# Gated MLP on transposed data: inverse roots broadcast through DRAM, the mean taken out of the first weights, and a reordered beginning

## The chip, the cores and the metric

The kernel runs on one core of a Trainium2 chip. The metric is the device time of one execution in microseconds (us), the median of three runs. The core has five engines with an instruction queue each: PE (TensorE, matmuls and transposes), DVE (VectorE), ACT (ScalarE), POOL (GpSimd) and SP (SyncE, which here only issues DMAs). Each engine works through its own queue in order, so an instruction that waits holds up everything queued behind it on that engine.

## The reference

The input x has 16 batches of 512 tokens with 128 features. A vector of modulations (scales, shifts, gates) is made from `c`. Cut to what matters:

```python
h = _layernorm(x) * (1 + ca) + sa
x = x + ga * _L0_attn_ref(h, ...)        # causal attention, 16 heads of 8
h = _layernorm(x) * (1 + cb) + sb
x = x + gb * _L0_ffn_ref(h, ...)         # the block below
# _L0_ffn_ref: two layers, each
x = x + local_attention(shift(x)) @ wo   # 8 heads of 64, window 64
h = shift_token(x)
mu, var = h.mean(-1), h.var(-1)
h = (h - mu) / sqrt(var + 1e-05) * lg + lb
a, g = split(h @ w1 + b1)                # 341 columns each
x = x + (a * gelu(g)) @ w2 + b2
```

The second half of each layer, from `mu, var` on, is called the MLP here. The first part of the change concerns it.

## The kernel before, in words

**Stage 1** (0 to about 640 us) is the causal attention, in units of a batch's heads, four units for each of the 16 batches. `stage_a` normalises a batch, transposes it, projects it to q and k, splits them into bf16 parts and writes these to DRAM (`qd`, `kd`; L269 is the line of all loads and stores that go through `load`). `load_stack` reads them back as the stacks `qst` and `kst`; rows 48 and 49 of each half of `kst` hold the constant −1, which `new_stack` sets with a memset of 32 rows (L486). `prep_mod`, `prep_gates` and the rest of `prep_...` make the modulations and the folded weights, in the order written out by hand ahead of the planner: batch 0's `stage_a` steps (`head[...]`) stand among them.

**Then two layers** (640 to 2008 us), each a local attention over the 16 batches (`proj_steps`, `chunk_steps`, `out_steps`) followed by the MLP over the 16 batches (`mlp_steps`). In layer 0 the attention takes about 640 to 1185 us and the MLP 1185 to 1305 us; in layer 1 the attention takes 1290 to 1865 us, and the MLP goes to the end.

**The residual stream** lies transposed in `ys`, 128 features on the partitions and 16 × 512 tokens along the free axis. The MLP's matmuls want their input this way, but mean and variance of a token are a reduction over partitions, so the kernel transposes:

- `stat_steps` (batches 0 to 13, beside the attention): four PE transposes, `bn_stats`/`bn_aggr` on DVE, and for every second batch an inverse root on ACT and POOL. It leaves mean and inverse root of each token as columns in SBUF.
- `mlp_steps`, step f1: four PE transposes of `ys` to tokens-on-partitions (L1197) and four DVE `tensor_scalar` of 128×128 that subtract the mean and multiply by the inverse root (L1188). For the last two batches (14 and 15, one pair) f1 makes the statistics too: transposes (L1209), `bn_aggr` (L1215), a bit trick for the inverse root on DVE (L1219 to L1221), three Newton rounds on POOL (12 small operations, L1225 to L1228), then the eight L1188 of both batches.
- f2: four PE transposes back (L1236), an ACT cast to the high part (L156), a DVE subtract for the low part (L1240).
- Three `gate` and three `up` steps (gelu on ACT; L1260 on DVE, a cast on ACT, L1265 on POOL), three `down` steps, then two DVE additions into `ys` (L1286). The last layer adds f5: scaling on ACT, four transposes (L1303), an addition of `x1` (L1305), the store of the output.

A product of full precision (`mm3`) is three fp32r matmuls of 128×512 (L867 to L869): high·high, high·low, low·high. A batch of the MLP has nine `mm3`, 27 matmuls.

**What sets the order.** `Plan.due(t, steps)` gives each step a due time, and the steps are emitted in order of these; the framework's scheduler then places the instructions on each engine. `MT` holds the due times of the MLP's steps in units of `UM` us from a batch's own start, `MTL` that of f1 of the late pair, `t1` the start of the MLP. Tiles from `flat("r")` and the like rotate through a fixed number of buffers (`FB`), `third(tag)` through three banks of PSUM, `ps_s()` through three others.

`weights_mlp` loads the MLP's weights, folds `ln_g` and `ln_b` into the first and splits them into high and low parts.

Of the kernel before, what the change touches and what calls it, by code (L numbers as in the profile page):

```python
# [35 lines left out]
LW, LWD = (2.8, 0.169)  # L36
LP0, LP1 = (-3.063, 0.706)

MT = (-2.0, -1.044, -0.081, 0.079, 0.264, 0.82, 0.69, 1.583, 0.71, 0.968, 1.97, 2.863)

EARLY, LS = 14, (0.3, 0.9)

MTL = -4.8

UA, UC, UM = (8.3, 8.033, 7.042)
GA, GM, GL = (0.037, 2.139, 0.75)

FB = (2, 2, 2, 2, 3, 6, 5, 4)
# [37 lines left out]
def kernel(  # L86
# [155 lines left out]
    for first in (False, True):  # L242
# [11 lines left out]
            nc.gpsimd.memset(m[0:64, 0:64], -NEG)  # L254
        masks.append(m)


    ys = const.tile([128, B, T + 1], F32, name="ys")
    nc.vector.memset(ys[64:128, :, 0:1], 0.0)
# [5 lines left out]
    wts = ctx.enter_context(tc.tile_pool(name="wts", bufs=1))  # L265
    weights = [{} for _ in range(DEPTH)]

    def load(**k):
        return tc.keep_in_program_order(nc.sync.dma_start(**k))  # L269

    def split(src, shape, name):
# [59 lines left out]
    def weights_mlp(l):  # L331
        W = weights[l]
        st_ = {}

        def f1():
            lg = wts.tile([128, 2], F32, tag="lg", name="lg")
            load(out=lg[:, 0:1], in_=ln_g[l].unsqueeze(1))
            load(out=lg[:, 1:2], in_=ln_b[l].unsqueeze(1))
            bb = W["b"] = wts.tile([128, 7], F32, tag="bb", name="bb")
            nc.gpsimd.memset(bb, 0.0)  # L340
            load(out=bb[:, 6:7], in_=b2[l].unsqueeze(1))
            for j in range(2):
# [12 lines left out]
        def g1():  # L355
            t, lg, bb = st_["1"], st_["lg"], W["b"]
            p = bank("m", BK[2])
            for i in range(6):
                nc.tensor.matmul(p[:, i : i + 1], lhsT=t[:, i, :], rhs=lg[:, 1:2], start=True, stop=True)
            nc.vector.tensor_tensor(bb[:, 0:6], bb[:, 0:6], p[:, 0:6], ALU.add)  # L360
            nc.vector.tensor_scalar(t, t, lg[:, 0:1], None, ALU.mult)
            W["1"] = split(t, [128, 6, 128], "w1")

        def f2():
            t = stage([128, 3, D])
            nc.gpsimd.memset(t, 0.0)
# [115 lines left out]
    def new_stack(i):  # L482
        q_ = at.tile([128, NH // 4, T], BF, name=f"qst{i}")
        k_ = at.tile([128, NH // 4, T], BF, name=f"kst{i}")
        for par in range(2):
            nc.gpsimd.memset(k_[64 * par + 32 : 64 * par + 64], -1.0)  # L486
        qst.append(q_)
        kst.append(k_)

# [36 lines left out]
    def stage_a(b):  # L526
# [29 lines left out]
        def put(key):  # L556
            def f():

                sp = s[key]
                d = dram.tile([6, HD, NH, T], BF, tag=key + "d", bufs=3, name=key + "d")  # L560
                for o, n, part in ((0, 3, 0), (3, 2, 1), (5, 1, 2)):
                    src = sp[:, 0:n] if key == "kd" else sp[:, part : part + 1].to_broadcast([128, n, T])
                    load(out=d[o : o + n].rearrange("s d h t -> (d h) s t"), in_=src)
                s[key] = d

            return f
# [19 lines left out]
    def load_stack(i):  # L586
        b, half = divmod(i, 2)
        for par in range(2):
            rows = slice(64 * par, 64 * par + R0)
            hs = slice(8 * par + 4 * half, 8 * par + 4 * half + 4)  # L590
            for st_, key in ((qst, "qd"), (kst, "kd")):
                load(out=st_[i % NS][rows], in_=st[b][key][:, :, hs, :].rearrange("s d h t -> (s d) h t"))

    def stacks(u):
        j = 2 * (u % 2)
# [553 lines left out]

    z_ = {}  # L1150

    mvs, rss = {}, {}

    def stat_steps(l, b):
        def f1():
            if b == 0:
                mvs[l] = small("lmv", [128, EARLY, NB, 2], 1)
            p = third("m")
            for n in range(NB):
                nc.tensor.transpose(p[:, n * 128 : (n + 1) * 128], ys[:, b, n * 128 : (n + 1) * 128], ident)  # L1160
            s6 = small("ms6", [128, NB, 6], 1)
            for n in range(NB):
                nc.vector.bn_stats(s6[:, n, :], p[:, n * 128 : (n + 1) * 128])
            for n in range(NB):
                nc.vector.bn_aggr(mvs[l][:, b, n, :], s6[:, n, :])

        def f2():
            if b % 2 == 0:
                return
            ve = small("lve", [128, 2, NB], 2)  # L1170
            nc.gpsimd.tensor_scalar(ve, mvs[l][:, b - 1 : b + 1, :, 1], EPS, None, ALU.add)
            rs, nwt = rsqrt_steps(pool["wk"], ve, [128, 2, NB], "ls", nc.gpsimd, EARLY // 2)
            for f in nwt:
                f()
            for i in range(2):
                rss[l, b - 1 + i] = rs[:, i, :]

        return [f1, f2]

    def mlp_steps(l, b):  # L1180
# [1 line left out]
        W = weights[l]  # L1182
        s = {}

        def normalised(p, b, mv, rs):
            z = z_[l, b] = flat("r").rearrange("p (n d) -> p n d", n=NB)
            for n in range(NB):
                nc.vector.tensor_scalar(  # L1188
                    z[:, n, :], p[:, n * 128 : (n + 1) * 128], mv[:, n, 0:1], rs[:, n : n + 1], ALU.subtract, ALU.mult
                )  # L1190

        def f1():
            if b < EARLY:

                p = ps_s() if b < 2 else third("e")
                for n in range(NB):
                    nc.tensor.transpose(p[:, n * 128 : (n + 1) * 128], ys[:, b, n * 128 : (n + 1) * 128], ident)  # L1197
                normalised(p, b, mvs[l][:, b], rss[l, b])
                return

            if b % 2 == 1:
                return
            s6 = small("mt6", [128, 2, NB, 6], 1)
            mv = small("mmv", [128, 2, NB, 2], 1)
            rs = small("mrs", [128, 2, NB], 1)
            ps = [third("e") for _ in range(2)]
            for i, p in enumerate(ps):
                for n in range(NB):
                    nc.tensor.transpose(  # L1209
                        p[:, n * 128 : (n + 1) * 128], ys[:, b + i, n * 128 : (n + 1) * 128], ident  # L1210
                    )
                for n in range(NB):
                    nc.vector.bn_stats(s6[:, i, n, :], p[:, n * 128 : (n + 1) * 128])
                for n in range(NB):
                    nc.vector.bn_aggr(mv[:, i, n, :], s6[:, i, n, :])  # L1215

            ve = small("mve", [128, 2, NB], 1)
            nt = small("mnt", [128, 2, NB], 1)
            nc.vector.tensor_scalar(ve, mv[:, :, :, 1], EPS, None, ALU.add)  # L1219
# [4 lines left out]
            for _ in range(3):  # L1224
# [1 line left out]
                nc.gpsimd.tensor_tensor(nt, nt, ve, ALU.mult)  # L1226
                nc.gpsimd.tensor_scalar(nt, nt, -0.5, 1.5, ALU.mult, ALU.add)
                nc.gpsimd.tensor_tensor(rs, rs, nt, ALU.mult)  # L1228
            for i, p in enumerate(ps):
                normalised(p, b + i, mv[:, i], rs[:, i])  # L1230

        def f2():
            p = ps_s() if b < 1 else third("e")
            z = z_.pop((l, b))
            for n in range(NB):
                nc.tensor.transpose(p[:, n * 128 : (n + 1) * 128], z[:, n, :], ident)  # L1236
            zh = flat("t1").bitcast(F32R)
            zl = flat("t2").bitcast(F32R)
            copy(11, zh, p)
            nc.vector.tensor_tensor(zl, p, zh.bitcast(F32), ALU.subtract)  # L1240
            s["zT"] = zh, zl

        def gate(i):
# [66 lines left out]
        steps = [f1, f2]  # L1310
        for i in range(3):
            steps += [gate(i), up(i)]
        steps += [down(i) for i in range(3)]
# [59 lines left out]
    for l in range(DEPTH):  # L1373
# [84 lines left out]
```

## Time and profile before

| what | value |
|---|---|
| median of 3 runs | 2010.7 us (2007.6 to 2011.55) |
| the profiled execution: its own time | 2010.06 us |
| its span, first to last instruction | 2008.3 us |
| mean granted PE clock over the span | 0.979 |
| stretch 640 to 1150 us (layer 0 attention) | PE 472.45, DVE 447.62, ACT 449.67 of 510.00 us |
| stretch 1185 to 1264 us (layer 0 MLP) | PE 78.34, DVE 58.42, ACT 48.61, POOL 49.54 of 79.00 us |
| stretch 1264 to 1277 us | PE 7.09 of 13.00 us, clock 0.75 |
| stretch 1885 to 1949 us (layer 1 MLP) | PE 64.00, DVE 51.52, ACT 44.72, POOL 30.03 of 64.00 us |
| stretch 1949 to 1964 us | PE 9.60 of 15.00 us, clock 0.77 |

The profiled execution has 1.76 us outside its span. A busy time is the time in which an engine was working, without the issuing of DMAs. Matmul durations overlap each other (one of 0.39 us is followed by the next after 0.23 us), so the cost of a matmul is read from the starts. In the rows of a timeline the columns are start, duration, engine, line, operation, output and inputs, shape and number merged into the row; in brackets stands how long the engine was idle before it and what ended that. SPq, DVEq and the like are the engines' queues: DMA issues and waits.

### The profile page before, as it was taken

How to read it: one execution, taken by the hardware profiler on the slowest of the kernel's cores; microseconds unless marked ns; L12 is line 12 of the kernel's file. 1: busy time of each engine (PE TensorE's matmuls, PEld its weight loads, DVE VectorE, ACT ScalarE, POOL GpSimd, SP SyncE). 2: the span in 40 equal slices, each digit the busy share in tenths (PEclk: the TensorE clock that was granted, in tenths of full speed). 3: DMA queues.
4: the chain of work that ended last, by engine and by line, in shares of the span. 5: the costliest groups of instructions: out<-in, count | busy, mean ns of one | idle time of the engine just before them, and what ended most of it. 6: DMA issues, size and time to landing. Idle time of an engine off the chain costs nothing. (4 is left out here: it accounts for less than half of the span.)

```text
span 2008.3 us, 55061 instructions
## 1 busy us (share of the span) xinstructions
PE 1810.0 (90%) x20474; PEld 1238.3 (62%) x20474; DVE 1631.2 (81%) x4851; ACT 1588.6 (79%) x4218; POOL 1319.2 (66%) x1916
## 2 busy tenths in 40 slices
PE   5899899898898799999999989889999899989998
PEld 3444444444444577777677768666767676767776
DVE  5788888888885888888888967698888888887686
ACT  2587777777787889999899875578889888888766
POOL 5345555555456878887878746587887777775444
PEclk8799999999999999999999999999999999999999
DMA  4445545545541211101010200020101010101022
GB/s 122 101 105 155 149 109 151 130 118 133 120 103 50 51 38 24 39 20 38 21 39 20 54 2 18 1 45 20 42 21 39 20 38 20 39 20 26 27 73 64
DMA packets 96904, 120.68 MB, mean 60 GB/s; under 512 B 16626, under 2 KB 79612, under 8 KB 94588
## 3 DMA queue, kind: packets, MB, share of 16 engines
q1 hardware_dynamic: 96156, 116.62, 24.1%
q8 instruction: 162, 2.65, 0.6%
q14 instruction: 106, 0.87, 0.1%
q10 hardware_dynamic: 480, 0.54, 0.1%
HBM read 48.43 MB, written 38.81 MB: 43 GB/s over the span
## 5 line engine op out<-in xcount | busy, mean ns | idle before, releaser
L174 ACT ACTIVATE pr<-pr,m 128x128 f32<-128x128 f32 x1024 | 408.9, 406 | 44.3 <-DVE m L1054 41.9
L627 DVE TENSOR_REDUCE mx<-ps_w 128x2 f32<-128x1024 f32 (+3 forms) x448 | 389.8, 911 | 62.2 <-PE ps_w L617 61.9
L953 POOL TENSOR_TENSOR r<-t,t 128x512 f32<-128x512 f32 x256 | 327.6, 1283 | 98.0 <-DVE t L944 65.2
L944 DVE TENSOR_TENSOR t<-ps_s,tab 128x512 f32<-128x512 f32 x512 | 327.8, 681 | 59.7 <-ACT sq L940 37.0
L174 ACT ACTIVATE pt<-ps_w 128x1024 f32<-128x1024 f32 x320 | 323.9, 1025 | 59.8 <-PE ps_w L706 55.4
L717 POOL TENSOR_SCALAR_AFFINE_SELECT pt<-pt 128x256 f32<-128x256 f32 (+1 forms) x448 | 190.7, 440 | 219.5 <-ACT pt L174 216.7
L1054 DVE CUSTOM_DVE_ANT_0 pr<-ps_e,maskl,rky 128x128 f32<-128x128 f32 x1024 | 295.5, 344 | 29.6 <-PE ps_e L1033 26.2
L1082 POOL TENSOR_TENSOR pr<-pr,den 128x512 f32<-128x512 f32 x256 | 265.6, 1041 | 76.7 <-DVE den L1081 70.3
L930 PE MATMUL ps_s<-wqh,hh 128*128 128x512 f32 x384 | 177.7, 463 | 36.2 <-DVE t L944 24.1
L174 ACT ACTIVATION_READ_ACCUMULATOR pr<-pr,m 128x1 f32 x1024 | 205.9, 201 | 0.0
L1265 POOL TENSOR_TENSOR kT<-pr,qT 128x512 fp32r<-128x512 f32 x96 | 123.0, 1292 | 121.5 <-ACT qT L156 121.2
L766 PE MATMUL ps_m<-pt,vau 128*32 128x512 f32 (+3 forms) x2048 | 197.4, 451 | 0.4 <-POOL pt L717 0.4
L1033 PE MATMUL ps_e<-kT,qT 64*64 64x128 f32 (+1 forms) x4608 | 180.1, 272 | 12.7 <-DVE m L1054 7.2
L950 DVE TENSOR_REDUCE ss<-sq 128x8 f32<-128x512 f32 x256 | 171.5, 675 | 2.1 <-ACT sq L940 2.1
L607 PE MATMUL ps_w<-kst,qst 48*128 48x512 bf16 (+3 forms) x1024 | 150.4, 310 | 21.3 <-ACT pt L174 11.3
L940 ACT ACTIVATE sq<-ps_s 128x512 f32<-128x512 f32 x256 | 150.1, 596 | 21.3 <-PE ps_s L932 17.1
L1033 PEld LDWEIGHTS ps_e<-kT,qT 64*64 64x64 f32 x4608 | 122.1, 133 | 68.1 <-issue 24.2
L706 PE MATMUL ps_w<-qst,kst 50*128 50x512 bf16 (+3 forms) x1024 | 126.4, 304 | 39.8 <-DVE mx L627 38.0
L931 PE MATMUL ps_s<-wql,hh 128*128 128x512 f32 x384 | 153.6, 400 | 0.0
L932 PE MATMUL ps_s<-wqh,hl 128*128 128x512 f32 x384 | 153.0, 399 | 0.0
L617 PEld LDWEIGHTS <-idm 64*128 64x128 bf16 x2048 | 103.8, 98 | 56.6 <-issue 26.7
L977 POOL TENSOR_TENSOR r<-r,rky 128x512 f32<-128x512 f32 x128 | 131.7, 1044 | 3.7
(244 smaller groups left out, 4244.9 us busy)
## 6 DMA issues: line engine op xcount, KB each, us to landing
v<-v SPq DMA_DIRECT2D x32, 512.0 KB
qst<-qdd SPq DMA_DIRECT2D x64, 192.0 KB
kst<-kdd SPq DMA_DIRECT2D x64, 192.0 KB
v<-v SPq DMA_DIRECT2D x32, 384.0 KB
qdd<-qd SPq DMA_DIRECT2D x16, 384.0 KB
kdd<-kd SPq DMA_DIRECT2D x16, 384.0 KB
od<-o SPq DMA_DIRECT2D x128, 36.0 KB
xt<-in_L_attn_x_dram SPq DMA_DIRECT2D x16, 256.0 KB
```

The costliest lines, as they stand in the source:

```text
L174: ins = nc.scalar.activation(*a, **k)
L627: nc.vector.tensor_reduce(dst, src, AX.X, ALU.max)
L717: nc.gpsimd.affine_select(v, v, pattern=[[0, n], [1, 128]], compare_op=ALU.is_ge, fill=0.0, base=0, channel_multiplier=-1)
L766: mm_ = nc.tensor.matmul(p[32 * hl : 32 * hl + 32, kb * 128 : T], lhsT=va[:, kb, h * 9 : h * 9 + 32], rhs=pts[hl, seg][:, off : off + n], ...
L930: nc.tensor.matmul(p, lhsT=hh[:, cols], rhs=wqh[:, wc], start=True, stop=False)
L931: nc.tensor.matmul(p, lhsT=hh[:, cols], rhs=wql[:, wc], start=False, stop=False)
L944: nc.vector.tensor_tensor(t, pv, W["tab"][:, n, 2 * j + k, :].unsqueeze(1).to_broadcast([128, LH, LD]), ALU.mult,)
L950: nc.vector.tensor_reduce(loc["ss"][:, n - n0, j, :], sq, AX.X, ALU.add)
L953: nc.gpsimd.tensor_tensor(r.rearrange("p h (x d) -> p h x d", x=2), t1.rearrange("p h (x d) -> p h x d", x=2), t2.rearrange("p h (x d) -> ...
L1033: nc.tensor.matmul(later["e"][64 * w : 64 * w + 64, par, hp * 128 + o : hp * 128 + o + n], lhsT=s["q"][r0 : r0 + 64, hp, q0 + 64 * w : q0 ...
L1054: nc.vector.tensor_tensor_reduce(pr[:, i, :], later["e"][:, par, hp * 128 : (hp + 1) * 128], mk, s["rq", cc][:, 2 * hp + par : 2 * hp + pa ...
L1082: nc.gpsimd.tensor_tensor(pr, pr, den.unsqueeze(2).to_broadcast([128, 4, 128]), ALU.mult)
```

## The change

1. **The MLP no longer transposes its input.** The mean of the tokens is removed by the weights: `weights_mlp` subtracts from each column of the folded first weights its mean over the 128 features (a matmul with a matrix of 1/128, two times 384 columns, and a DVE subtraction each). What remains per token is a factor, the inverse root. `put_roots` writes it to DRAM (`rsd`, one row of 512 per batch) with one DMA per batch from SP, in single elements of 4 bytes. f1 is now a DMA that reads the row back, broadcast to 128 partitions (256 KB, into `flat("sq")`, which has two buffers); f2 is one DVE product of 128×512 of `ys` and this tile, then the cast and the subtraction as before, now from SBUF.
2. **The statistics of the late pair** move into a new step f0 with the due time `MTL`; its inverse roots go through DRAM like the others. Its `z` is made in f2, no longer with the statistics.
3. **Due times and buffers:** the first entry of `MT` goes from −2.0 to −3.0, `UM` from 7.042 to 6.0, `t1` is bounded by f0 of the late pair; `up` takes its bank from `third("e")` from batch 2 on.
4. **The beginning:** the eight memsets of `kst` on POOL become eight small DMAs from SP of two rows each; `new_stack` and `head[0]` (normalisation of batch 0) go ahead of `prep_silu` and `prep_mod`, `head[5]` and `head[6]` (projections, `qd`/`kd`) ahead of `prep_mod(2, 5)` and `prep_gates`; for batch 0 the writes of `kd` and the loads of `kst` are issued by ACT.

```diff
-MT = (-2.0, -1.044, -0.081, 0.079, 0.264, 0.82, 0.69, 1.583, 0.71, 0.968, 1.97, 2.863)
+MT = (-3.0, -1.044, -0.081, 0.079, 0.264, 0.82, 0.69, 1.583, 0.71, 0.968, 1.97, 2.863)
-UA, UC, UM = (8.3, 8.033, 7.042)
+UA, UC, UM = (8.3, 8.033, 6.0)
...
+    ones = const.tile([128, 128], F32, name="ones")
+    nc.gpsimd.memset(ones, 1.0 / D)
...
             nc.vector.tensor_scalar(t, t, lg[:, 0:1], None, ALU.mult)
+            for j in range(2):
+                p = bank("m", BK[2])
+                tj = t[:, 3 * j : 3 * j + 3, :].rearrange("p i n -> p (i n)")
+                nc.tensor.matmul(p[:, 0:384], lhsT=ones, rhs=tj, start=True, stop=True)
+                nc.vector.tensor_tensor(tj, tj, p[:, 0:384], ALU.subtract)
             W["1"] = split(t, [128, 6, 128], "w1")
...
         for par in range(2):
-            nc.gpsimd.memset(k_[64 * par + 32 : 64 * par + 64], -1.0)
+            nc.sync.dma_start(
+                out=k_[64 * par + R0 : 64 * par + R1], in_=minus.unsqueeze(1).to_broadcast([2, NH // 4, T])
+            )
...
-                    load(out=d[o : o + n].rearrange("s d h t -> (d h) s t"), in_=src)
+                    load(b == 0 and key == "kd", out=d[o : o + n].rearrange("s d h t -> (d h) s t"), in_=src)
...
+    def put_roots(l, b, rs):
+        for i in range(2):
+            nc.sync.dma_start(out=rsd[l][b + i].rearrange("(n p) -> p n", p=128), in_=rs[:, i, :])
...
-        def normalised(p, b, mv, rs):
-            z = z_[l, b] = flat("r").rearrange("p (n d) -> p n d", n=NB)
-            for n in range(NB):
-                nc.vector.tensor_scalar(
-                    z[:, n, :], p[:, n * 128 : (n + 1) * 128], mv[:, n, 0:1], rs[:, n : n + 1], ALU.subtract, ALU.mult
-                )
-        def f1():
-            if b < EARLY:
-                p = ps_s() if b < 2 else third("e")
-                for n in range(NB):
-                    nc.tensor.transpose(p[:, n * 128 : (n + 1) * 128], ys[:, b, n * 128 : (n + 1) * 128], ident)
-                normalised(p, b, mvs[l][:, b], rss[l, b])
+        def f0():
+            if b < EARLY or b % 2 == 1:
                 return
+            for i in range(2):
+                variance(l, b + i, third("e"))
...
-            for i, p in enumerate(ps):
-                normalised(p, b + i, mv[:, i], rs[:, i])
+            put_roots(l, b, rs)
+
+        def f1():
+            s["rs"] = flat("sq")
+            nc.sync.dma_start(out=s["rs"], in_=rsd[l][b].unsqueeze(0).to_broadcast([128, T]))
         def f2():
-            p = ps_s() if b < 1 else third("e")
-            z = z_.pop((l, b))
-            for n in range(NB):
-                nc.tensor.transpose(p[:, n * 128 : (n + 1) * 128], z[:, n, :], ident)
+            z = flat("r")
+            nc.vector.tensor_tensor(z, ys[:, b, 0:T], s["rs"], ALU.mult)
             zh = flat("t1").bitcast(F32R)
             zl = flat("t2").bitcast(F32R)
-            copy(11, zh, p)
-            nc.vector.tensor_tensor(zl, p, zh.bitcast(F32), ALU.subtract)
+            copy(11, zh, z)
+            nc.vector.tensor_tensor(zl, z, zh.bitcast(F32), ALU.subtract)
...
-                p = ps_s()
+                p = ps_s() if b < 2 else third("e")
...
+    minus = pp.tile([2, T], BF, name="minus")
+    nc.gpsimd.memset(minus, -1.0)
     if B > 1:
         load_x(1)
+    for i in range(NS):
+        new_stack(i)
     head = stage_a(0)
+    head[0]()
     prep_silu()
     prep_mod(0, 2)
-    head[0]()
     prep_q()
     prep_k()
     for f in head[1:4]:
         f()
+    head[5]()
+    head[6]()
     prep_mod(2, 5)
     prep_gates()
-    head[5]()
-    head[6]()
-    for i in range(NS):
-        new_stack(i)
...
-        t1 = max(t0 + 4 * B * UC + GM, freed - UM * (B - 1 + MT[0]) + 0.1)
+        t1 = max(t0 + 4 * B * UC + GM, freed - UM * (B - 2 + MTL) + 0.1)
-            for t, f in zip(MT, lazy(lambda l=l, b=b: mlp_steps(l, b), 11 + int(last))):
-                due(t1 + UM * (b + (t if b < EARLY or t != MT[0] else MTL)), [f])
+            for t, f in zip((MTL,) + MT, lazy(lambda l=l, b=b: mlp_steps(l, b), 12 + int(last))):
+                due(t1 + UM * (b + t), [f])
```

`variance(l, b, p)` holds the four transposes, `bn_stats` and `bn_aggr` that `stat_steps` and the late pair had written out. In the loads of `load_stack`, `b == 0 and key == "kd"` is passed in the same way, and `load(True, ...)` issues from ACT.

More of the change, by code (lines that the diff above doesn't have):

```diff
@@ L266, with load @@
     weights = [{} for _ in range(DEPTH)]
-    def load(**k):
+    def load(other=False, **k):
+        if other:
+            return nc.scalar.dma_start(**k)
         return tc.keep_in_program_order(nc.sync.dma_start(**k))
@@ L591, in load_stack @@
             for st_, key in ((qst, "qd"), (kst, "kd")):
-                load(out=st_[i % NS][rows], in_=st[b][key][:, :, hs, :].rearrange("s d h t -> (s d) h t"))
+                load(b == 0 and key == "kd", out=st_[i % NS][rows], in_=st[b][key][:, :, hs, :].rearrange("s d h t -> (s d) h t"))
     def stacks(u):
@@ L1150, with variance @@
     z_ = {}
-    mvs, rss = {}, {}
+    rsd = [dram.tile([B, T], F32, name=f"rsd{l}") for l in range(DEPTH)]
+    mvs = {}
+    def put_roots(l, b, rs):
+        for i in range(2):
+            nc.sync.dma_start(out=rsd[l][b + i].rearrange("(n p) -> p n", p=128), in_=rs[:, i, :])
+    def variance(l, b, p):
+        if b % 2 == 0:
+            mvs[l, b] = small("lmv", [128, 2, NB, 2], 2)
+        mv = mvs[l, b - b % 2][:, b % 2]
+        for n in range(NB):
+            nc.tensor.transpose(p[:, n * 128 : (n + 1) * 128], ys[:, b, n * 128 : (n + 1) * 128], ident)
+        s6 = small("ms6", [128, NB, 6], 2)
+        for n in range(NB):
+            nc.vector.bn_stats(s6[:, n, :], p[:, n * 128 : (n + 1) * 128])
+        for n in range(NB):
+            nc.vector.bn_aggr(mv[:, n, :], s6[:, n, :])
     def stat_steps(l, b):
         def f1():
-            if b == 0:
-                mvs[l] = small("lmv", [128, EARLY, NB, 2], 1)
-            p = third("m")
-            for n in range(NB):
-                nc.tensor.transpose(p[:, n * 128 : (n + 1) * 128], ys[:, b, n * 128 : (n + 1) * 128], ident)
-            s6 = small("ms6", [128, NB, 6], 1)
-            for n in range(NB):
-                nc.vector.bn_stats(s6[:, n, :], p[:, n * 128 : (n + 1) * 128])
-            for n in range(NB):
-                nc.vector.bn_aggr(mvs[l][:, b, n, :], s6[:, n, :])
+            variance(l, b, third("m"))
         def f2():
@@ L1170, in f2 @@
             ve = small("lve", [128, 2, NB], 2)
-            nc.gpsimd.tensor_scalar(ve, mvs[l][:, b - 1 : b + 1, :, 1], EPS, None, ALU.add)
-            rs, nwt = rsqrt_steps(pool["wk"], ve, [128, 2, NB], "ls", nc.gpsimd, EARLY // 2)
+            nc.gpsimd.tensor_scalar(ve, mvs.pop((l, b - 1))[:, :, :, 1], EPS, None, ALU.add)
+            rs, nwt = rsqrt_steps(pool["wk"], ve, [128, 2, NB], "ls", nc.gpsimd, 2)
             for f in nwt:
                 f()
-            for i in range(2):
-                rss[l, b - 1 + i] = rs[:, i, :]
+            put_roots(l, b - 1, rs)
         return [f1, f2]
@@ L1183, in mlp_steps @@
         s = {}
-        def normalised(p, b, mv, rs):
-            z = z_[l, b] = flat("r").rearrange("p (n d) -> p n d", n=NB)
-            for n in range(NB):
-                nc.vector.tensor_scalar(
-                    z[:, n, :], p[:, n * 128 : (n + 1) * 128], mv[:, n, 0:1], rs[:, n : n + 1], ALU.subtract, ALU.mult
-                )
-        def f1():
-            if b < EARLY:
-                p = ps_s() if b < 2 else third("e")
-                for n in range(NB):
-                    nc.tensor.transpose(p[:, n * 128 : (n + 1) * 128], ys[:, b, n * 128 : (n + 1) * 128], ident)
-                normalised(p, b, mvs[l][:, b], rss[l, b])
+        def f0():
+            if b < EARLY or b % 2 == 1:
                 return
[L1201 to L1204, printed above, removed]
+            for i in range(2):
+                variance(l, b + i, third("e"))
+            ve = small("lve", [128, 2, NB], 2)
+            nt = small("mnt", [128, 2, NB], 1)
             rs = small("mrs", [128, 2, NB], 1)
-            ps = [third("e") for _ in range(2)]
-            for i, p in enumerate(ps):
[L1208 to L1219, printed above, removed]
+            nc.vector.tensor_scalar(ve, mvs.pop((l, b))[:, :, :, 1], EPS, None, ALU.add)
             nc.vector.tensor_scalar(nt.bitcast(I32), ve.bitcast(I32), 1, None, ALU.logical_shift_right)
@@ L1228, in f1 @@
                 nc.gpsimd.tensor_tensor(rs, rs, nt, ALU.mult)
-            for i, p in enumerate(ps):
-                normalised(p, b + i, mv[:, i], rs[:, i])
+            put_roots(l, b, rs)
+        def f1():
+            s["rs"] = flat("sq")
+            nc.sync.dma_start(out=s["rs"], in_=rsd[l][b].unsqueeze(0).to_broadcast([128, T]))
         def f2():
-            p = ps_s() if b < 1 else third("e")
-            z = z_.pop((l, b))
-            for n in range(NB):
-                nc.tensor.transpose(p[:, n * 128 : (n + 1) * 128], z[:, n, :], ident)
+            z = flat("r")
+            nc.vector.tensor_tensor(z, ys[:, b, 0:T], s["rs"], ALU.mult)
             zh = flat("t1").bitcast(F32R)
             zl = flat("t2").bitcast(F32R)
-            copy(11, zh, p)
-            nc.vector.tensor_tensor(zl, p, zh.bitcast(F32), ALU.subtract)
+            copy(11, zh, z)
+            nc.vector.tensor_tensor(zl, z, zh.bitcast(F32), ALU.subtract)
             s["zT"] = zh, zl
@@ L1308, in f5 @@
             )
-        steps = [f1, f2]
+        steps = [f0, f1, f2]
         for i in range(3):
```

## The prediction

> **What bounds the kernel now.** I read the page's busy shares first, then a table by stage, because the shares are a mean over stages with different limits.
>
> ```profile
> PE 1810.0 (90%) x20474; PEld 1238.3 (62%) x20474; DVE 1631.2 (81%) x4851; ACT 1588.6 (79%) x4218; POOL 1319.2 (66%) x1916
> ```
>
> PE leads, but only by 9 points. Four slices of 7 us, as columns length, PE, PEld, DVE, ACT, POOL, granted clock, DMA share and GB/s, say more:
>
> ```profile
> 1178.00:1185.00 7.00, 4.12 (x65) 3.34 (x66) 4.04 (x21) 6.14 (x22) 2.41 (x3) 1.00 0.01 2
> 1206.00:1213.00 7.00, 7.00 (x34) 5.70 (x33) 4.69 (x7) 4.60 (x7) 2.27 (x3) 1.00 0.00 0
> 1220.00:1227.00 7.00, 7.00 (x36) 5.73 (x35) 6.89 (x14) 4.54 (x8) 4.83 (x5) 1.00 0.03 7
> 1269.00:1276.00 7.00, 3.79 (x12) 2.71 (x13) 4.63 (x13) 0.58 (x1) 0.67 (x4) 0.61 0.00 0
> ```
>
> In the MLP (rows 2 and 3) PE is full, so removed PE work is removed time. In the passage from attention to MLP (row 1) nothing is full: a chain of DVE, ACT, POOL and PE. At the late pair (row 4) PE stands and its clock falls. These three places, and the first 40 us, are what the change touches.
>
> **1. Transposes out of a full PE.** The timeline of PE in layer 0:
>
> ```profile
> 1246.84 0.39 PE L868 MATMUL ps_m<-kT,w2h 128*128 128x512 f32 x1
> 1247.07 0.39 PE L869 MATMUL ps_m<-qT,w2l 128*128 128x512 f32 x1
> 1247.30 0.60 PE L1209 MATMUL ps_x<-ident,ys 128*128 128x128 f32 x4
> 1247.65 0.48 PE L867 MATMUL ps_s<-t,w1h 128*128 128x512 f32 x1
> 1247.97 0.39 PE L868 MATMUL ps_s<-t,w1h 128*128 128x512 f32 x1
> ```
>
> A matmul costs 0.23 us from start to start. Four transposes and the matmul after them take 1247.30 to 1247.97, 0.67, so four transposes cost 0.44 and one 0.11. A batch of layer 0 is now 27 × 0.233 + 8 × 0.11 = 7.18 us, and 6.30 after; layer 1 (four more transposes in f5) goes from 7.62 to 6.74. Removed per layer are 14 × 8 + 2 × 4 = 120 transposes; I leave out the 16 of batches 0 and 1, which fall in the unfilled passage. So 2 × 104 × 0.11 = **−23 us**, −26 if all count.
>
> It holds only if no other engine is near 6.3. DVE per batch loses four L1188 of 0.40 (1.6 in sum, 1.37 pipelined) and gains one product of 128×512 in f32, which is nearest to L1240 (0.69): 0.69 + 0.69 + 3 × 0.75 (L1260) + 2 × 0.75 (L1286) = 5.1, and 5.8 with L1305 in layer 1. ACT: 3 × 0.68 (gelu) + 3 × 0.62 + 0.58 = 4.5, about 6.0 with f5. POOL 3 × 1.29 = 3.9. All are below 6.30 and 6.74, but DVE and ACT in layer 1 by little; were they the bound by queueing, half of the gain would go (−11).
>
> **2. The late pair.** Its L1188 wait for POOL's Newton rounds:
>
> ```profile
> 1269.95 1.37 DVE L1188 TENSOR_SCALAR r<-ps_x,mmv,mrs 128x128 f32<-128x128 f32 x4 [2.59 <-POOL mrs L1228]
> ...
> 1271.38 1.12 PE L1197 MATMUL ps_x<-ident,ys 128*128 128x128 f32 x4 [3.94 <-DVE r L1188]
> ...
> 1273.80 0.58 ACT L156 CAST t<-ps_e 128x512 fp32r<-128x512 f32 x1 [8.50 <-PE ps_e L1236]
> ```
>
> The bracket of row 1 names POOL, of row 2 the DVE queue behind it: an earlier batch's L1188 stands behind the late pair's eight, so PE starves and restarts slow. In 1264 to 1277 PE issues 23 instructions: 10 transposes and 13 matmuls, worth 1.1 + 3.0 = 4.1 us at full clock, so 8.9 of 13 us are lost. In 1949 to 1964 (layer 1) 34 instructions, 16 and 18, are worth 6.0: 9.0 of 15 lost. Together 17.9.
>
> After the change the DVE instruction that waits is the pair's product `z`, and between inverse root and `z` there are more links. In the order of the new kernel's DVE seven operations (about 5.1 us) stand between the bit trick (`nt`, `rs` in f0) and `z` of batch 14 in layer 0, ten (7.4 us) in layer 1. The chain: 1.3 until POOL starts (1265.3 to 1266.6) + 3.3 Newton + two put issues 0.7 + landing 1.5 + a load 2.9 + its issue 0.4, about 10 us. The bounds of the unknown links are these rows, two of stage 1's DRAM trip and one of the last chain:
>
> ```profile
> 318.40 0.34 SPq L269 DMA_DIRECT2D rdd<-rd  x1
> ...
> 319.87 0.59 SPq L269 DMA_DIRECT2D rb<-rdd  x1
> ```
>
> ```profile
> 2001.47 2.87 DMA v<-x1d
> ```
>
> A write to DRAM had landed by 1.5 us after its issue, and a load of the same 256 KB took 2.87. So DVE stalls 5 us in layer 0 and 3 in layer 1; PE has 2 to 4 us of matmuls queued, and loses about 3 and 1: 17.9 − 4 = **−14 us** (−17 if covered, −5 if both stalls reach PE in full and the clock falls).
>
> The clock: PE idle 3.94 us here, granted 0.61 in the slice, matmuls 0.43 apart. The Trainium skill (TensorE: Matmul & The Clock Gate, Part 1) puts the fall to half clock after an idle window of about 3.4 us. By it my 3 us in layer 0 keep the clock with little room; past it a dozen matmuls 0.43 apart in place of 0.23 would add 2.4.
>
> **3. The beginning.** The timeline, first POOL and DVE, then SP's queue, then the first use of scores:
>
> ```profile
> 4.33 14.85 POOL L486 MEMSET kst<- 32x2048 bf16 x8
> 14.70 2.74 DVE L522 TENSOR_SCALAR xn<-xt,mv,rsy 128x128 f32<-128x128 f32 x4
> ```
>
> ```profile
> 26.80 0.32 SPq L473 DMA_DIRECT2D gad<-ga  x1
> 27.22 1.57 SPq L269 DMA_DIRECT2D qdd<-qd  x3
> ```
>
> ```profile
> 39.68 3.55 DVE L627 TENSOR_REDUCE mx<-ps_w 128x2 f32<-128x1024 f32 x4 [3.16 <-PE ps_w L617]
> ```
>
> The x of batch 0 has its first `bn_stats` at 5.21, its last at 11.6, behind the modulations' chain; then L522 takes 2.74 beside POOL's memsets (1.11 for batch 1 without them). `qd` is ready at 23.8 but its write waits behind `gad` until 27.2, and the first `kst` load goes at 33.4. With `head[0]` first, no memsets and no `gad` ahead, I put `hT` at 12 (18.2 now), the writes at 20 to 21, the loads' end at 26, first maximum at 27 to 30. That is −10 to −12; but batch 1's projections, which now come behind the first scores on PE, and ACT, which now issues seven DMAs (0.3 to 0.6 each by SP's rows), may give some back, and so may PE's clock, granted 0.50 from 40 to 70. I take **−9 us** (−12 to −4). Everything in stage 1 then moves by that.
>
> The Trainium skill speaks against part of it: DMA: Bandwidth & Descriptors (Issuing engines are not separate DMA queues) says that a second issuing engine saves only the issue time. No run here shows two at once on this path; by it ACT's seven issues are worth no more than the 3 us or so that they took on SP.
>
> **4. What the DRAM trip costs in the passage.** `z` of batches 0 to 7 stands on DVE between the last attention chunks, in order. A load into `sq` can be issued only when the `z` two batches before is done, and lands 3.3 us later (0.4 + 2.9); on SP it also stands behind the next layer's 768 KB of weights (layer 0) and the puts of pair 12/13. Where `z` waits, the chunk's L1054 behind it waits, then ACT's exp, then the gelu, which cannot start until the last exp. Below: nothing, or a gain of 2.7 (batches 0 and 1 lose their L1188, 1.37 each). Above: two waits of 3.3 a layer and a slow put, 7 a layer. I take **+8 us** for both layers, nearer the upper end, since row 1 of the slices shows no engine with work to spare there (bounds −3 to +14).
>
> **5. Additions.** Two products with `ones` per layer, f32, 384 columns: a pair of f32 products of 512 columns took 2.07 in the beginning (at low clock), so at most 0.8 each, and two subtractions of about 0.55 on DVE, which delay the weights' split; +0 to +3, I take **+2**. Sixteen loads and puts per layer run where the DMA share is 0.0 to 0.25. SP holds nothing else that is urgent there but the output stores of layer 1. A put is 512 runs of 4 bytes per batch, where stage 1's was of 256 bytes; no row of before has that at size, so its landing may be twice the 1.5 us, which is in the bounds of steps 2 and 4.
>
> **Sum.** −23 − 14 − 9 + 8 + 2 = −36. From the profiled execution's own 2010.06 that is 1974; the median of the runs is 0.6 above, hence **1975 us**. All bounds at their good end give −26 − 17 − 12 − 3 = −58 (1953); all at their bad end −11 − 5 − 4 + 14 + 3 = −3 (2007).
>
> **Rivals.**
>
> *The trip through DRAM gives half of it back (1992).* For it: DVE works in order, two buffers, SP's queue, the short passage. Then the passage costs +14 and the late pair saves only 5 with the head at −8: −23 − 5 − 8 + 14 + 3 = −19, from 2010.06 to 1991, by the median 1992, some 1985 to 2000. Against: in steady state a load has two periods, 12.6 us, for 3.3.
>
> *Slower.* One mechanism: the loads through two `sq` buffers become a chain that paces the MLP. `z` of a batch waits for a load that is issued after the `z` two before, so the period cannot be less than half of issue-to-use. It decides from 12.6 us per trip; at 2 × 7.8 = 15.6 the batches take 1.5 us more than my 6.30, 32 × 1.5 = 48 against the 36 saved: 2022. A trip of 3.3 by the rows above would have to be almost five times as long, by small puts or SP's queue. Unlikely.
>
> *Another engine takes over (1986).* DVE or ACT in layer 1 by queueing, or the banks that `up` now shares with the statistics: −11 in place of −23 gives 1986.
>
> *The MLP doesn't gain at the end* since its last batches wait for attention's last: excluded, the last attention output is long done when PE is full at 1206.
>
> **Chances.** Forecast (1962 to 1984) 0.62; half given back 0.16; another engine 0.12; slower 0.07; the rest, within 0.2% (4 us, about what a measurement of this kernel can tell from no change), 0.03. The 8-in-10 range leaves out the slower case and the tails: 1957 to 1999. Faster by over 0.2%: 0.90; within: 0.03; slower: 0.07.
>
> **What would show it.** Right: first L627 before 31; a table by stage with PE full in both MLPs and 6.3 and 6.7 us between the additions into `ys`; at the late pair a gap of PE under the 3.94 us of now and the clock near 1.00; in the passage waits of DVE for the DMA of `sq`, 3 us at most. Wrong: periods over 7 with DVE waiting on `sq`; a PE gap at the late pair as long as before; L627 early but the second batch's scores late.

## The result, and the profile after

The changed kernel takes 2039.4 us (median of 4 runs, 2038.1 to 2042.2) against 2009.5 of the kernel before (4 runs, 2007.6 to 2011.55): a ratio of 1.015, 95% interval 1.0133 to 1.0168. It is slower by 30 us where 36 us less were forecast. The profiled execution has a span of 2037.9 us.

Where the time went is read first from milestones in the traces (us from the span's start; `den` is the reciprocal that each half of a local attention chunk takes on DVE, `ys` the first of the two additions of the MLP's last batch into the residual stream). The last two columns are experiments told of below. Stage 1 alone, of the same instructions, ends up to 9.2 us apart between traces, and a later stage varies by some 3 us, so differences of that size say little.

| milestone | before | changed | `after_put32` | `rows` |
|---|---|---|---|---|
| first maximum of the scores | 39.7 | 32.9 | 33.2 | 32.5 |
| last maximum of stage 1 (its start) | 612.8 | 605.4 | 606.6 | 604.2 |
| last `den`, layer 0 | 1183.2 | 1216.0 | 1193.2 | 1180.4 |
| last batch's `ys`, layer 0 | 1320.4 | 1354.4 | 1321.6 | 1306.0 |
| last `den`, layer 1 | 1864.0 | 1894.2 | 1845.6 | 1839.4 |
| end | 2008.3 | 2037.9 | 1981.6 | 1970.7 |

The changed kernel is 7.4 us ahead when stage 1 ends, and 32.8 behind when the attention of layer 0 ends. Its two MLPs, from the last `den` on, take 138.4 and 143.7 us against 137.2 and 144.3: no gain is seen there, though the transposes are gone.

The page of the changed kernel, busy times of the engines, then a table by stage (columns as in the prediction):

```profile
PE 1802.6 (88%) x20242; PEld 1222.6 (60%) x20242; DVE 1623.6 (80%) x4759; ACT 1587.1 (78%) x4218; POOL 1320.1 (65%) x1910
```

```profile
640.00:1150.00 510.00, 457.89 (x5507) 348.39 (x5507) 426.82 (x1589) 431.32 (x1459) 391.54 (x498) 0.97 0.15 31
1185.00:1220.00 35.00, 22.97 (x285) 17.52 (x284) 15.88 (x75) 21.64 (x75) 8.90 (x11) 0.80 0.27 62
1293.00:1312.00 19.00, 10.79 (x44) 7.75 (x43) 6.41 (x12) 6.97 (x12) 7.85 (x16) 0.90 0.11 29
1972.00:1992.00 20.00, 10.05 (x40) 6.71 (x37) 8.28 (x12) 7.59 (x12) 7.13 (x10) 0.80 0.55 53
```

In 640 to 1150, where only attention runs, every engine is less busy than before (PE 457.89 against 472.45, DVE 426.82 against 447.62) although its instructions there are nearly the same: they wait more. The other rows are the passage of layer 0 and the two late pairs, with PE idle for 8 to 12 us in each.

What they wait for at a late pair is told by the chain of waits in layer 1 (start, duration, what):

```profile
1973.63 0.21 POOL mrs L1226
...
1973.86 10.68 DMA rsd<-mrs
...
1984.56 3.45 DMA sq<-rsd
```

The load (3.45) is near the 2.87 that the prediction took; the write of 2 × 512 roots takes 10.68 us, where the prediction took 1.5. At the late pair of layer 0 the issues of the write and of the next load stand at 1297.19 and 1307.72, 10.53 apart. The waits that follow, first DVE's, then PE's:

```profile
1195.48 0.69 DVE L1235 TENSOR_TENSOR r<-ys,sq 128x512 f32<-128x512 f32 x1 [6.62 <-DMA sq<-rsd]
...
1310.97 1.29 DVE L1235 TENSOR_TENSOR r<-ys,sq 128x512 f32<-128x512 f32 x2 [10.02 <-DMA sq<-rsd]
...
1875.64 0.69 DVE L1235 TENSOR_TENSOR r<-ys,sq 128x512 f32<-128x512 f32 x1 [7.17 <-DMA sq<-rsd]
```

```profile
1989.56 0.79 PE L881 MATMUL ps_e<-t,w1h 128*128 128x512 f32 x1 [9.14 <-DVE pr L1259]
```

Rows 1 and 3 are the passages, behind the write of pair 12/13; row 2 is the late pair.

In the attention nothing waits for a root, and yet time goes. The place of one of the seven writes in layer 0, on SP, PE and DVE:

```profile
961.18 0.92 SPq L1171 DMA_DIRECT2D rsd<-lsy  x2
975.88 0.47 SPq L1020 DMA_DIRECT2D v<-v  x1
```

```profile
967.64 0.56 PE L1125 MATMUL ps_m<-pT,v 128*64 128x64 f32 x10
969.33 0.22 PE L1125 MATMUL ps_m<-pT,v 128*64 128x64 f32 x1 [1.13 <-issue]
972.45 0.27 PE L1125 MATMUL ps_m<-pT,v 128*64 128x64 f32 x1 [2.90 <-issue]
```

```profile
972.66 0.35 DVE L1068 CUSTOM_DVE_ANT_0 pr<-ps_e,maskl,rky 128x128 f32<-128x128 f32 x1 [4.20 <-remote]
```

PE stops in the middle of a group of matmuls, with no releaser that the profile shows ("issue"), and DVE behind it, 7 to 11 us after the write of the roots. In the same stretch PE's instruction fetch (16 KB by a DMA of its own) begins at 966.84 and takes 3.24 us, by the trace's DMA packets; the median of these fetches is 1.04. It ends at 970.08, and PE goes on only at 972.45. This made the first theory.

### The profile page after: what moved, and what is told of

Its sections match the earlier page's. It is cut to its first block, busy times and chain, and to the rows that moved or that the text cites. A ratio compares the mean times of both kernels' runs of the same rounds, so it can differ in the third digit from the quotient of the medians.

```text
span 2037.9 us, 54591 instructions
## 1 busy us (share of the span) xinstructions
PE 1802.6 (88%) x20242; PEld 1222.6 (60%) x20242; DVE 1623.6 (80%) x4759; ACT 1587.1 (78%) x4218; POOL 1320.1 (65%) x1910
## 5 line engine op out<-in xcount | busy, mean ns | idle before, releaser
L1264 POOL TENSOR_TENSOR kT<-pr,qT 128x512 fp32r<-128x512 f32 x96 | 130.9, 1377 | 112.5 <-ACT qT L156 108.5
L954 ACT ACTIVATE sq<-ps_s 128x512 f32<-128x512 f32 x256 | 150.8, 597 | 21.2 <-PE ps_s L946 16.1
```

## Experiments

**Theory 1:** the write of the roots in single 4-byte elements is slow to land, about 10 us, and while it is under way engines that have nothing to do with it are held up as well, through PE's instruction fetch among other things. **Theory 2:** the write only delays those who read it; the attention is slower because the scheduler put its instructions in another order.

### The write alone, in the kernel before: `before_put4`, `before_put32`

Both add to the end of `stat_steps` a write of the roots to a spare tile in DRAM that nobody reads. For `before_put4`, twice per pair, with i = 0 and 1:

```diff
+                nc.sync.dma_start(out=spare[l][b - 1 + i].rearrange("(n p) -> p n", p=128), in_=rs[:, i, :])
```

and for `before_put32`, one per pair:

```diff
+            nc.sync.dma_start(
+                out=spare[l][b - 1 : b + 1].rearrange("i t -> (i t)").rearrange("(p k) -> p k", p=128),
+                in_=rs.rearrange("p i n -> p (i n)"))
```

> The kernel before, which also writes the inverse roots of each statistics pair to a spare DRAM tile that nobody reads: two DMAs of 512 single 4-byte elements per pair, seven pairs per layer, as the changed kernel does; PE, DVE, ACT and POOL keep their order word for word. Theory 1 (the small writes hold up other DMAs for about 10 us each, PE's instruction fetch and the loads of v among them): slower by 15 to 45 us, most of it in the attention of layer 0 (the profile of the change lost about 30 us there), with instruction fetches of over 3 us behind the writes. Theory 2 (the attention of the changed kernel is slower because its instructions stand in another order): within 4 us of 2010.

> As the run before, but the same 4 KB of a pair leave in one DMA of 128 runs of 32 bytes. Theory 1 in the form that the number of runs matters (1024 against 128): an eighth of the delay, so within 5 us of 2010. If a write under 512 bytes costs whatever its number: as slow as the run with 4-byte runs. Theory 2: within 4 us of 2010.

Measured: 2041.95 us with 4-byte runs, ratio 1.015 (1.0125 to 1.0175); 2010.3 with 32-byte runs, ratio 0.9998 (0.9985 to 1.0012). The same 4 KB per pair, the same order of PE, DVE, ACT and POOL, and nobody reads them: 14 pairs' writes of touching words cost 31 us. By the milestones the two attentions take 17.7 and 12.5 us longer than with 32-byte runs, and the two MLPs change by less than 0.5. Theory 2 has fallen as an explanation of most of the loss. DVE of `before_put4` after the first write, first SP's issue, then DVE:

```profile
771.76 0.93 SPq L1178 DMA_DIRECT2D spare<-lsy  x2
```

```profile
777.05 0.69 DVE L1123 TENSOR_TENSOR ol<-ps_m,oh 128x512 fp32r<-128x512 f32 x1 [0.91 <-ACT v L156]
782.00 0.35 DVE L1054 CUSTOM_DVE_ANT_0 pr<-ps_e,maskl,rky 128x128 f32<-128x128 f32 x1 [4.26 <-PE ps_m L988]
```

The same two instructions in `before_put32`:

```profile
773.92 0.69 DVE L1123 TENSOR_TENSOR ol<-ps_m,oh 128x512 fp32r<-128x512 f32 x1 [0.91 <-ACT oh L156]
774.60 0.35 DVE L1054 CUSTOM_DVE_ANT_0 pr<-ps_e,maskl,rky 128x128 f32<-128x128 f32 x1
```

The 4.26 us stand before an instruction whose scores PE had finished at 777.7; the releaser that the row names ended at 780.8. Instruction by instruction, PE's lag behind the run with 32-byte runs has grown, 20 us after each of the seven writes of layer 0, by 4.8, 3.4, 1.1, 0.0, 3.6, 1.5 and 4.7 us, and it changes by 0.6 us at most from there to 50 us after the write.

The same trace speaks against the instruction fetch as the way in which most of this time goes. A fetch of over 2.5 us stands beside the second, fourth and sixth of these writes only. The three dearest, the first, fifth and seventh, have none, and the fourth has one of 3.63 us and costs nothing.

### The changed kernel with its roots in 32-byte runs: `after_put32`

```diff
-        for i in range(2):
-            nc.sync.dma_start(out=rsd[l][b + i].rearrange("(n p) -> p n", p=128), in_=rs[:, i, :])
+        nc.sync.dma_start(
+            out=rsd[l][b : b + 2].rearrange("i t -> (i t)").rearrange("(p k) -> p k", p=128),
+            in_=rs.rearrange("p i n -> p (i n)"))
```

The roots then stand in DRAM in another order than f1 reads them, so this kernel computes something else; it serves for its time alone.

> The changed kernel with its roots written in one DMA of 128 runs of 32 bytes per pair; the roots then stand in another order in DRAM, so tokens get one another's factors; PE, DVE, ACT and POOL keep the order of the changed kernel word for word. Theory 1: landing falls from about 10.5 us to 2 or so, the stalls of the attention, of the passage (DVE 6.6 us in layer 0, 7.1 in layer 1) and of the late pairs (8 us each less) go: 1975 to 1995 us. Theory 2: only the passage and the late pairs gain, 2010 to 2025 us.

Measured: 1982.5 us, ratio to the kernel before 0.986 (0.9831 to 0.9888). With the order of the changed kernel, the write alone decides between 30 us more and 28 us less than before. By the table of milestones it is worth 57.5 us after stage 1: 24.0 in the attention of layer 0 and its passage (605.4 to 1216.0 against 606.6 to 1193.2), 10.0 in the MLP of layer 0, 15.8 in layer 1's attention, 7.7 in its MLP.

Not all that layer 0's attention lost was the write. With the cheap write it still takes 16.1 us longer than in the kernel before (587 against 570), 11.5 of them from the 96th `den` to the last, while layer 1's attention takes 19.6 less. So the other order of the instructions, theory 2, does move the attentions, in both directions.

The late pair of layer 1 on SP, write and loads:

```profile
1926.82 0.33 SPq L1170 DMA_DIRECT2D rsd<-mrs  x1
1928.27 0.98 SPq L1233 DMA_DIRECT2D sq<-rsd  x2
```

1.45 us in place of 10.7, about what the prediction had assumed. At the late pair of layer 0 it is 3.63; over all 16 writes of this run the landing has a median of 1.43 and goes up to 4.05.

### One small transpose ahead of the write: `rows`, `rows_early`

```diff
     def put_roots(l, b, rs):
...
+        p = third("m")
+        nc.tensor.transpose(p[0:8, 0:128], rs.rearrange("p i n -> p (i n)"), ident)
+        row = small("row", [8, 128], 1)
+        nc.scalar.copy(row, p[0:8, 0:128])
+        nc.sync.dma_start(out=rsd[l][b : b + 2].rearrange("i (n p) -> (i n) p", p=128), in_=row)
...
```

It is called in a step of its own, 0.6 units of 8.033 us after the Newton rounds (for the late pair one period after f0). `rows_early` has `MTL = -9.0`.

> The changed kernel with its roots turned on PE first: a pair's 128x8 roots are transposed to 8x128, copied by ACT and written as 8 runs of 512 bytes, each in a step of its own behind the Newton rounds; the loads are as in the changed kernel and every token gets its own factor. Theory 1 (number of small runs): as good as the run with 32-byte runs, 1980 to 1990 us (the scheduler places some 2400 of 14100 rows of PE elsewhere, worth a few us either way). If a transpose on PE and a copy on ACT per pair cost what the small writes cost: above 2000.

> As the run before, with the statistics of the late pair due 4.2 periods earlier (MTL -9.0 in place of -4.8). If the late pair's chain (Newton rounds, write, load) is what is left of the gap there (intervals of 12.9 and 11.0 us against some 7 with 32-byte runs): 6 to 10 us under the run before. If the pair's gap is now other work (banks, ACT): no difference over 3 us.

Measured: `rows` 1977.7 us, ratio 0.9844 (0.9827 to 0.986), the fastest of all here and 61.7 under the changed kernel; `rows_early` 1982.4, ratio 0.9866 (0.9852 to 0.9881). `rows` is 2 us under the range that was expected. The earlier statistics gain nothing (4.7 us slower, with intervals of the ratios that overlap), which fits that `rows` has no gap left at the late pair: PE in the stretches around it, and, in layer 1, the load that follows the write 1.39 us later (2.20 in layer 0):

```profile
1264.00:1272.00 8.00, 8.00 (x35) 6.00 (x34) 5.30 (x7) 5.60 (x11) 6.74 (x6) 1.00 0.19 67
1922.00:1930.00 8.00, 8.00 (x39) 6.32 (x38) 6.32 (x9) 6.83 (x12) 5.38 (x4) 1.00 0.58 166
```

```profile
1923.82 0.29 SPq L1174 DMA_DIRECT2D rsd<-row  x1
1925.21 1.00 SPq L1242 DMA_DIRECT2D sq<-rsd  x2
```

The intervals of the additions into `ys` at that place are 8.0 and 7.7 us, where the kernel before had 19.4 and 19.3.

### What the removed transposes are worth: `rows_transposes`

```diff
                 p = ps_s()
+                for n in range(2 * NB if i == 0 else 0):
+                    k = 128 * (n % NB)
+                    nc.tensor.transpose(p[:, k : k + 128], ys[:, b, k : k + 128], ident)
                 mm3(p, W["1"][0][:, 3 + i, :], W["1"][1][:, 3 + i, :], zh, zl, True, True)
```

> The kernel with rows of 512 bytes, and eight PE transposes of ys per batch of the MLP put back ahead of the first gate's matmuls, into the bank that these overwrite: PE's work of before without the rest of it (no DVE normalisation, no transposes of its result that anything waits for). If PE bounds the MLP, as the prediction's first step has it: 32 batches x 8 x 0.11 = 28 us slower than without them at most, 23 with the first batches hidden: 1998 to 2006. If PE has room there (start gaps of 0.5 to 1 us per batch in layer 1): 5 to 15 us slower, 1983 to 1993.

Measured: 1992.3 us, 14.6 more than `rows` by the medians, which lies in the range expected if PE has room in the MLP, not in that of a PE that bounds it. In the traces the two MLPs, from the last `den` on, take 7.5 and 14.3 us longer, 21.8 together. The two attentions, whose instructions were placed anew, take 2.0 and 3.6 less; the rest of the difference of the spans (22.7) is stage 1, 6.6 us later in this execution with the same instructions. A stretch of 65 us in the MLP of layer 1, `rows` and then `rows_transposes`:

```profile
1885.00:1950.00 65.00, 62.59 (x281) 47.57 (x279) 50.27 (x85) 49.20 (x80) 37.71 (x39) 1.00 0.29 82
```

```profile
1893.00:1958.00 65.00, 61.97 (x306) 48.22 (x305) 47.66 (x77) 43.06 (x69) 34.63 (x36) 1.00 0.26 71
```

PE is as full in both (62.59 and 61.97 of 65.00), and less of the other engines' work gets done where it transposes (ACT 43.06 against 49.20). This run prices the transposes in the new order only: it has PE's work of the kernel before without the gap at the late pair, and yet its two MLPs (133.1 and 145.5) are together only 2.8 us shorter than those of before (137.2 and 144.3). What the new order or the new due times cost there, no run tells.

### The beginning alone: `head_only`

The kernel before with part 4 of the change and nothing else.

> The kernel before with the reordered beginning alone. The first maximum came 6.8 us earlier in the changed kernel and the gain stood at 7.4 us when the first attention ended; if nothing later takes it back: 2002 to 2004 us. Rival: the layers' other order (the scheduler places the later instructions anew) eats or adds some us: 1998 to 2012.

Measured: 1997.1 us, ratio 0.9924 (0.9896 to 0.9953), 13.7 under the kernel before and under both ranges that were expected. The first maximum stands at 32.8, as in the changed kernel, 6.9 us earlier. How the rest of the gain comes about is not shown: the profiled execution is the slowest of the four (1996.4 to 2002.6), its stage 1 ends 1.6 us before that of the kernel before, and what follows, whose instructions were placed anew, takes 5.8 us less.

### What makes the write dear: `put32x1024`, `put4_apart`, `put4_one`, `put4_16`, `put4_8`

All are the kernel before with one extra DMA per pair of 1024 runs that nobody reads, and they differ in the length of the runs and their distance in DRAM. The destination of `put4_apart`, in rows of 16 words (`put32x1024` has `0:8` in place of `0:1` and a source read eight times):

```diff
+                out=spare[l][b // 2].rearrange("(p r) c -> p r c", p=128)[:, :, 0:1],
```

that of `put4_one`:

```diff
+                out=spare[l][b // 2].rearrange("n p -> p n"),
```

and that of `put4_16` and `put4_8`, where c has 4 and 2 words:

```diff
+                out=spare[l][b // 2].rearrange("n p c -> p n c")[:, :, 0:1],
```

> The kernel before with one extra DMA per pair of 1024 runs of 32 bytes (the roots eight times over) into rows 64 bytes apart, read by nobody; all engines but SP in the order of before. If the number of runs sets the cost: as slow as 4-byte runs, 2035 to 2045 us. If the cost lies in many 4-byte writes into the same line of DRAM: within 6 us of 2010.

> As the run before, with 1024 runs of 4 bytes, each alone in its 64 bytes of DRAM. Number of runs: 2035 to 2045 us. Neighbouring 4-byte writes into one line: within 6 us of 2010.

> The kernel before with one extra DMA per pair of 1024 runs of 4 bytes that lie side by side in DRAM, neighbours from neighbouring partitions, as the changed kernel's two DMAs write them; read by nobody, all engines but SP in the order of before. If neighbouring words in one line of DRAM make the cost: as slow as with two DMAs, 2035 to 2045 us. If the second DMA or its queueing made it: under 2020.

> As the run before, with the words 16 bytes apart, four in 64 bytes instead of sixteen. If the writes into one line of 64 bytes go one after the other (about 10.5 us for sixteen, so 0.65 each): a landing of some 2.6 us, little or nothing to be seen, 2006 to 2018 us. If a line is longer than 64 bytes or any sharing is dear: 2030 or more.

> As the run with words 16 bytes apart, with 8 bytes. By the semaphore updates of the traces a write of 1024 words side by side lands after 9 to 11 us, of words 16 or 64 bytes apart after 3.0 to 3.8. The theory of writes that go one after the other in a line of 64 bytes has thereby fallen: four words in a line cost nothing. If the cost begins where two words share some unit under 16 bytes: landing well over 4 us, and 2020 to 2035 us. If only words that touch are dear (a write that is merged or split with its neighbour): landing of 3 to 4 us, and 2008 to 2018 us.

Landing is read from the updates of the DMA semaphores in the trace, from the issue to the last one recorded, as a median where all 16 updates of a write are there; writes that another issue follows closely are left out. Behind touching words most writes have fewer than 16 (in `put4_one` one of 14 has all), and there the last update recorded is taken, as a range. Fetches are the instruction fetches over 2.5 us after 640 us, of some 185.

| run | runs × bytes, distance | lands after (us) | long fetches | ratio to before (interval) |
|---|---|---|---|---|
| `before_put32` | 128 × 32, touching | 1.40 | 0 | 0.9998 (0.9985 to 1.0012) |
| `put32x1024` | 1024 × 32, 64 bytes | 2.45 | 0 | 0.9998 (0.9978 to 1.0017) |
| `put4_apart` | 1024 × 4, 64 bytes | 3.30 | 0 | 1.0011 (0.9999 to 1.0022) |
| `put4_16` | 1024 × 4, 16 bytes | 3.09 | 0 | 1.0009 (0.999 to 1.0027) |
| `put4_8` | 1024 × 4, 8 bytes | 4.17 | 0 | 1.0007 (0.9992 to 1.0021) |
| `put4_one` | 1024 × 4, touching | 8 to 11 | 8 | 1.0159 (1.0129 to 1.0189) |
| `before_put4` | 2 × 512 × 4, touching | 8 to 11 | 7 | 1.015 (1.0125 to 1.0175) |

So it is neither the number of runs (1024 of 32 bytes cost nothing that can be measured) nor their length by itself (nor do 1024 of 4 bytes, 8 bytes apart), nor the second DMA (`put4_one` has only one). My expectation that sixteen writes go one after the other in a line of 64 bytes fell with `put4_16`, where four share it and land no later than one: the cost sets in where the 4-byte words touch (words 8 bytes apart land a little later, after 4.17, and cost nothing either). In all these writes neighbours in DRAM come from neighbouring partitions; touching words from one partition were not run. The packets themselves do not differ in the traces: in `put4_8` (write at 831.5) and `put4_one` (at 836.6) the 1024 packets of 4 bytes are recorded from 0.91 to 1.60 us after the issue in both, and the last recorded update of the semaphore comes 3.88 us after it in the one and 10.70 in the other. So the extra time lies behind the recorded packets; why, and where, stays open.

Also open is how an engine is held while such a write is under way. Eight of the fetches of the changed kernel take over 2.5 us (up to 3.9) and none of `after_put32`; but the fetches don't account for most stops, as told above, and DVE's stop at 777.7 in `before_put4` has no fetch beside it that lasts over 1.5 us. The trace itself has holes there: where words do not touch, each of these writes shows 16 semaphore updates, and behind touching words often only some of them are recorded. Releasers named in such a stretch ("issue", "remote", an instruction long over) are not to be trusted. No run was made that could tell these apart.

## Why the prediction was wrong, step by step

**The step that failed** is the price of one term, in two places. In step 2, "a write to DRAM had landed by 1.5 us after its issue" was taken from a write with runs of 256 bytes and used for one of touching 4-byte words; step 5 named the difference and put it at "twice the 1.5 us, which is in the bounds". It is 10.5 us, seven times. And step 5 let the puts beside the attention cost nothing, because the DMA share there is under 0.25: in `before_put4` such puts cost 31 us with nobody reading them, nearly all of it beside the attention. The profile could not price this, since before had no such write; the honest bound would have been open upwards, and with 14 writes beside a chain of four engines it was the largest unknown of the sum. The forecast's rival "slower" had the right object, a trip through DRAM, and the wrong place: the loads' pace in the MLP. The load that is in the chain came in 3.45 us, and away from the late pair the pace of the MLP was no slower than before (the other 14 intervals between the additions of layer 0 sum to 99.6 us, before to 100.1); the write was the slow part, and most of what it cost lies in the attentions (24 and 16 of the 57.5 us).

The Trainium skill (DMA: Bandwidth & Descriptors, Rules for kernel authors) has a rule against this very write: a last dimension that is not contiguous becomes one descriptor per element, and should be rearranged. The traces agree on the number, 1024 packets of 4 bytes per pair, and following the rule gives `rows`. The rule names no price, and the number is not the price here: 1024 packets of one element, 8 bytes apart, cost nothing that these runs can measure.

**Step 1, the transposes, −23:** put back into `rows`, they cost 21.8 us inside the two MLPs, 14.6 net. Taken out of the kernel before, they are not seen at that size, even where the write is cheap: in `after_put32` the 14 intervals of each layer between the additions into `ys`, without the one at the late pair, sum to 97.1 and 98.1 us, in `rows` to 97.8 and 96.4, and before to 100.1 and 99.6. That is 4.5 and 5.5 us gained in both layers together, and an interval of about 7.0 us in place of 7.1, where 6.3 and 6.7 were forecast. So −23 is not confirmed; either the new order gives most of it back, or PE did not bound the MLP alone.

**Step 2, the late pair, −14:** the intervals there became 19.9 and 20.3 (before 19.4 and 19.3), so +1.5. With 32-byte runs they are 12.9 and 11.0, together 14.8 less than before, and in `rows` 8.0 and 7.7, together 23.0 less. The chain was rightly listed, and its landing was mis-sized. Clock and gap in the changed kernel: PE 9.14 us idle and a granted clock of 0.80 in 1972 to 1992, where the forecast had a gap under 3.94 and a clock near 1.00.

**Step 3, the beginning, −9:** the first maximum came 6.8 us earlier, the end of stage 1 7.4; inside the bounds, though the sign named for it, a first maximum before 31, did not come. As a mean over all traces stage 1 ends at 614.1 with the old beginning and at 608.4 with the new one, 5.7 earlier. `head_only` as a whole gained 13.7 (9.5 to 20.9 by its interval), over the good bound of 12.

```profile
32.92 1.22 DVE L641 TENSOR_REDUCE mx<-ps_w 128x2 f32<-128x1024 f32 x1 [6.26 <-PE ps_w L631]
```

**Step 4, the passage, +8:** in the changed kernel DVE waits there 6.62 and 7.17 us at one `z` of each layer, behind the write of pair 12/13. With the cheap write of `after_put32`, its lead over the kernel before goes from 1.6 us at the 96th `den` of layer 0 to −10.0 at the last, and in layer 1 from 14.8 to 18.4: +11.5 and −3.6, which together meet the +8, but in neither layer. In `rows` it goes from 5.8 to 2.8 and from 21.9 to 24.6: +3.0 and −2.7.

**The sum** was forecast at 1975; with the same instructions on PE, DVE, ACT and POOL and a write that lands in 1.4 us at the median the kernel takes 1982.5, and `rows` 1977.7. One price, too low by a factor of seven, makes 57.5 of the 64 us between forecast and result. But that the totals come so close without it is in part luck. What each stage takes more (+) or less (−) than in the kernel before, in us:

| stage | `after_put32` | `rows` |
|---|---|---|
| stage 1 | −6.2 | −8.6 |
| attention of layer 0 | +16.1 | +5.8 |
| MLP of layer 0 | −8.8 | −11.6 |
| attention of layer 1 | −19.6 | −10.2 |
| MLP of layer 1 | −8.3 | −13.1 |

Steps 1 and 2 forecast 37 us out of the MLPs, where 17.1 and 24.7 came; and layer 1's attention, which the forecast had at nothing but its share of the passage, gave what was missing.

## What to carry to other kernels

Price a DMA from a row of the same shape, with the same run length and the same distance between runs; where no such row exists, the bound is open, and a cheap remedy is to change the shape (here one small transpose, so that 128 roots leave as one run). A DMA that nobody waits for can still be paid for by everybody: 4 KB per pair, unread, cost 31 us, and neither its bytes nor its share of the queues showed that. Of the writes tried, only those that landed late (8 to 11 us) cost anything. And test a suspect write by itself, in the old kernel, with nobody reading it: one line told apart what the two traces could not.

## What the runs showed of the hardware

- 1024 words of 4 bytes written side by side into DRAM, neighbours from neighbouring partitions, land after 8 to 11 us, 8 bytes apart after 4.2, 16 or 64 bytes apart after 3.1 to 3.3; 1024 runs of 32 bytes after 2.45, 128 of them after 1.4. The packets of touching words and of words 8 bytes apart are recorded over the same 0.91 to 1.60 us (`put4_one` at 836.6, `put4_8` at 831.5).
- While touching words are under way, some instruction fetches of 16 KB took up to 3.9 us in the changed kernel and 4.6 in `put4_one`, in place of 1.0 to 1.1, and PE and DVE stopped for 2.9 and 4.3 us (rows above) where the trace names no releaser or one that was long done. Most of the stops have no long fetch beside them.
- Stage 1 of the same instructions ends at 608.8 to 618.0 us in the traces of the kernels with the old beginning, and at 604.2 to 612.1 in those with the new one: a gain of 7 us at the beginning is of the size of that spread.
